# Rows outside, columns inside: another order of the elements in the tiles of h

## The chip, the cores and the metric

The kernel runs on one core of a Trainium2 chip. The metric is the device time of one execution in microseconds (us); lower is better. The kernel before takes 1774.77 us, the median of three runs between 1773.58 and 1776.81 us. Engines are written as in the profile: PE is the matrix engine (PEld its weight loads), DVE the vector engine, ACT the scalar engine, POOL the GpSimd engine, SP the engine whose queue issues most DMAs.

## The reference

Two layers act on x of shape (16, 64, 128, 128), which is 16 images of 64 channels and 128 x 128 pixels.

```python
# layer 0: a Hartley transform cut to 20 x 20 modes, mixed by w1, turned back, blurred, masked
x_ht = dht_2d(x)
out_ht = zeros.at[:, :, :20, :20].set(compl_mul2d(x_ht[:, :, :20, :20], w1))
x = gaussian_smoothing_4d(dht_2d(out_ht) / (H * W)) * mask
# layer 1
h = _group_norm(x, gn1_w, gn1_b)
h = _afno(h, ...) + x            # Fourier transform, 32 x 32 modes, two small layers, back
residual = h
feats = _gelu(_c1(_group_norm(h, gn2_w, gn2_b), fe_w, fe_b))
out = sum over 2 shared layers of _gelu(_c1(feats, shared_w[s], shared_b[s])) / 2
gate_w = top 4 of 16 experts, from feats.mean(axis=(2, 3)) through a small network
for e in range(16):
    out = out + _gelu(_c1(feats, expert_w[e], expert_b[e])) * gate_w[:, e]
return out + residual
```

`_c1` is a 64 x 64 product over the channels, the same for each pixel. The kernel computes only the four experts that each image's gate picks.

## The kernel before

**Ahead of the images.** Layer 0 and the spectrum of layer 1 are worked out in the space of modes, for all 16 images, in about the first 525 us (lines 208 to 658). Nothing there touches h. One table made there matters below: `edges` (line 555) writes, for each image, the 4 rows at either end of a column whose blur is cut by the border; its table `edge` is made on the host in `constant_tables`.

**The images, one after the other.** In the second part, image b goes through these steps, each on tiles of 128 partitions x 2 x 512 numbers of 32 bits. The 128 partitions are 64 channels of the upper and 64 of the lower half of the image's rows; one tile holds 16 columns of 64 rows each, 1024 numbers in a partition, and eight tiles (`NSL`) make an image.

- `columns` (line 713): four calls; PE turns the spectrum into columns in PSUM, and ACT copies it to `u` (line 728). That copy reads PSUM with a step of 64 numbers, 16 at a time, and writes runs of 8.
- `pixels` (line 733): eight calls; PE makes the pixels, one matmul per column (line 744), so that a PSUM tile lies column by column: 16 columns (s, j), with 64 rows i inside. `evacuate` copies it to a tile of `h`. For t in `BY_ACT` = (0, 2, 4, 6) ACT does this (line 754), for the others DVE (line 756). For t below 5 DVE adds the edge rows (line 758); at t = 1 and 3 the DVE copy leaves out the first 4 rows, since line 758 reads them from PSUM itself.
- `feature` (line 804): PE multiplies h by the feature weights (line 814), ACT applies Gelu (line 818).
- `gate` (line 824): a chain of small steps on PE, ACT and DVE from the sums of the features to the four experts' weights; POOL computes the softmax's power (line 877) and fetches the chosen weights with indirect DMAs (line 884).
- `group` / `expert` (line 895): 48 calls for an image, 2 shared layers and 4 experts by eight tiles. PE multiplies (line 904), ACT applies Gelu to a tile `g` (line 909), and DVE adds `g` times its share to `h` in place (line 913). In the last expert (`last`, 8 of the 48) DVE writes the sum to `stg` instead (line 919), a tile of a whole image: [128, 64 rows, 128 columns], row by row as the output has it.
- `store` (line 935): after the last tile of an image SP issues the DMAs that write `stg` out; for the last image this is done after each two tiles. There is one `stg`.

**What sets the order.** PE, ACT and DVE run in the order in which the program issues. That is written out by hand: `PIECES` gives, for each step of image b, its place among the 48 groups of image b and of those before it. So, while the groups of image b run, `columns` (but for its first call, which is among the groups of image b - 1), `pixels` and `feature` of image b + 1 are issued between them. In each group's code the ACT part is put off by one step (`on_act`) and the DVE part by one more (`on_dve`). The buffers: three PSUM tiles `pe` (pool ps2), 13 of `h`, 10 of `f`, 7 of `g`.

The last image's groups have no next image's steps between them.

**The views before.** `evacuate` and the last addition see h and g column by column:

```python
hv, pv = (v.rearrange("p s (j i) -> p (s j) i", i=C) for v in (h, ps))     # line 750
gv, hv = (v.rearrange("p s (j i) -> p (s j) i", i=C) for v in (g, h))      # line 918
box["out"][:, :, c0:c0 + 16].rearrange("p i m -> p m i"),                  # line 920
```

so line 919 reads g and h as they lie and writes 64 rows' elements of one column after another, each 128 numbers (512 bytes) from the one before.

Of the kernel before, what the change touches and what calls it, by code (L numbers as in the profile page):

```python
# [13 lines left out]
ALU = mybir.AluOpType  # L14
# [4 lines left out]
NB, C, N = 16, 64, 128  # L19
K = 20  # L20
# [10 lines left out]
EC = 65  # L31
# [25 lines left out]
def constant_tables():  # L57
# [21 lines left out]
    e1, e2 = blur @ e, mask[:, None] * (blur @ e)  # L79
# [5 lines left out]
    ends = n[:64], np.concatenate([n[124:], n[64:124]])  # L85
# [6 lines left out]
            inv2[r:r + 32, j], inv2[r + 32:r + 64, j] = np.cos(a32)[:, ns], -np.sin(a32)[:, ns]  # L92
    e_cols = np.concatenate([np.stack([s_[:32].reshape(4, 8) for s_ in sides], 1).ravel(), [32]])
    d1 = e1 - g1 * e
    edge = np.zeros((K, K, 2, EC, 4))
    for k2 in range(K):
        for k1 in range(K):
            for j in range(2):
                edge[k2, k1, j] = (np.outer(e2[e_cols, k2], d1[ends[j][:4], k1]).real
                                   - np.outer(e2[e_cols, k2 + 1], d1[ends[j][:4], k1 + 1]).imag)  # L100

# [24 lines left out]
    def by_parity(v):  # L128
        v = v.reshape(K // 2, 2, K, *v.shape[2:])
        return np.ascontiguousarray(np.moveaxis(v, (1, 2, 0), (0, 1, 2)))  # L130
# [6 lines left out]
    def chunked(a):  # L137
        a = a.reshape(4, CH, -1)
        return a.transpose(1, 0, 2)

    sel = np.zeros((CH, K, 2, 32))
    for k1 in range(K):
# [5 lines left out]
    at = np.arange(128)  # L148
# [7 lines left out]
    out = {  # L156
        "fwd1": fwd1,
        "fwd2": fwd2.reshape(N, 2 * K * W1),
        "inv1": inv1.reshape(128, -1),
        "inv2": inv2.reshape(128, -1),  # L160
        "edge": chunked(by_parity(edge).reshape(NM, 2 * EC * 4)).reshape(CH, -1),
        "gain": np.broadcast_to(g1[1:] / g1[:K], (128, K)),
        "spec": chunked(spec.reshape(NM, 2 * MD * MD)),
        "dev": chunked(dev.T.copy()),
# [13 lines left out]
def hartley_afno_moe_kernel(ctx: ExitStack, tc: tile.TileContext, a: dict, out: bass.AP):  # L178
    nc = tc.nc
# [5 lines left out]
    def load(pool, name, shape, eng=None):  # L185
        t = pool.tile(shape, F32, name=name + "_sb", tag=name)
        src = a[name]
        if len(shape) == 3 and len(src.shape) == 2:
            src = src.rearrange("p (a b) -> p a b", b=shape[2])
        (eng or nc.sync).dma_start(t, src)  # L190
        return t
# [16 lines left out]
    with tc.tile_pool(name="modes", bufs=1) as mp:  # L208
# [6 lines left out]
        with tc.tile_pool(name="f_x", bufs=10) as xp, tc.tile_pool(name="f_t", bufs=2) as tp, \  # L215
# [45 lines left out]
            for b in range(NB):  # L261

                t1 = tp.tile([P, 2 * K, C], F32, name="t1")
                for c0 in range(0, C, 8):
                    xt = xp.tile([P, 8, N], F32, name="xt")
                    nc.sync.dma_start(xt, a["x"][b, :, c0:c0 + 8])
                    ps = pp1.tile([P, 8, W1], F32, name="ps1")
# [18 lines left out]
        with tc.tile_pool(name="m_o", bufs=1) as op, tc.tile_pool(name="m_w", bufs=4) as wp, \  # L286
# [16 lines left out]
            edge = load(sc, "edge", [CH, 4, 2 * EC * 4])  # L303
# [7 lines left out]
            for h in range(2):  # L311
                hs_ = slice(h * CL, (h + 1) * CL)
                for ri in range(2):
                    own_rows = slice(h * C + ri * CL, h * C + (ri + 1) * CL)
                    for ro in range(2):
                        c0 = (ri ^ ro) * P + h * CL
# [14 lines left out]
            for k1 in range(K // 2 + 1):  # L331

                ps = pp.tile([P, K // 2, 2, NB, 2], F32, name="psm")
# [15 lines left out]
            for b0 in range(0, NB, 8):  # L349
                for cc in range(2):  # L350
                    pq = [pp2.tile([CH, 8, C], F32, name="pst") for h in range(2)]
                    for i in range(8):
                        for h, (m0, m1) in ((0, (0, C)), (1, (C, CH)), (1, (0, C)), (0, (C, CH))):
                            g = slice(h * C, (h + 1) * C)
# [62 lines left out]
    with tc.tile_pool(name="s_o", bufs=1) as so, \  # L417
# [27 lines left out]
        for g, cols in halves:  # L445
            sq = sqp.tile([CH, 4, 512], F32, name="sq")
            sqs.append(sq)
            for rc in range(4):
                ps = pp2.tile([P, 512], F32, name="psx")
# [17 lines left out]
        gm, gd, gv, y, t = (small(n, HG) for n in ("gm", "gd", "gv", "gy", "gt1"))  # L467
# [36 lines left out]
        for r in range(4):  # L504
            g = slice(r * CL, (r + 1) * CL)
            c0 = (r & 1) * C + (r >> 1) * CL
# [19 lines left out]
        for q in range(4):  # L526
            g = slice(q * 32, (q + 1) * 32)
            i = q % 2 * QB * C
# [98 lines left out]
        for b in range(NB):  # L627
            xk = sw.tile([P, MD * MD], F32, name="xk")
            xr = sw.tile([P, MD * MD], F32, name="xr")
            for n in range(2):  # L630
                cols = slice(n * 512, (n + 1) * 512)
                ps = pp2.tile([P, 512], F32, name="psx")
# [30 lines left out]
    with s3:  # L663
# [14 lines left out]
        def on_act(f):  # L678
            behind_a.append(f)

        def on_dve(f):
            behind_d.append(f)
            while len(behind_d) > 1:
                behind_d.popleft()()
# [5 lines left out]
        def flush():  # L690
            done(0)
            while behind_d:
                behind_d.popleft()()
# [39 lines left out]
        def pixels(box, t):  # L733


            if t == 0:
                if box["columns"] < 4:
                    flush()
                box["h"] = []
            ps = ps2.tile([P, 2, 512], F32, name="pe")  # L740
            for j in range(8):
                for s, half in ((0, 0), (1, 1), (0, 1), (1, 0)):
                    rs = slice(s * C, (s + 1) * C)
                    nc.tensor.matmul(ps[half * C:(half + 1) * C, s, j * C:(j + 1) * C],  # L744
                                     lhsT=u[rs, t * 8 + j], rhs=inv2[rs, half], start=True, stop=True)

            def evacuate():
                h = hpp.tile([P, 2, 512], F32, name="h")
                box["h"].append(h)
                hv, pv = (v.rearrange("p s (j i) -> p (s j) i", i=C) for v in (h, ps))  # L750
                nm = min(16, EC - 16 * t)
                at = 4 if t < 4 and t not in BY_ACT else 0
                if t in BY_ACT:
                    nc.scalar.copy(h, ps)
                else:
                    nc.vector.tensor_copy(hv[:, :, at:], pv[:, :, at:])  # L756
                if nm > 0:
                    nc.vector.tensor_tensor(hv[:, 0:nm, 0:4], (pv if at else hv)[:, 0:nm, 0:4],  # L758
                                            box["edge"].rearrange("p (m i) -> p m i", i=4)[:, 16 * t:16 * t + nm],
                                            ALU.add)  # L760

            on_act(evacuate)

# [133 lines left out]
        def expert(box, t, w, bias, share, last=False):  # L897
            if box["features"] <= t:
                flush()
            f, h = box["f"][t], box["h"][t]  # L900
            ps = ps2.tile([P, 2, 512], F32, name="pe")
            for p, half in ((0, 0), (1, 1), (0, 1), (1, 0)):
                rows_ = slice(p * C, (p + 1) * C)
                nc.tensor.matmul(ps[half * C:(half + 1) * C, p], lhsT=w[rows_],  # L904
                                 rhs=f[rows_, half], start=True, stop=True)

            def activate():
                g = gp.tile([P, 2, 512], F32, name="g")
                nc.scalar.activation(g, ps, AF.Gelu, bias=bias)  # L909

                def add():
                    if not last:
                        nc.vector.scalar_tensor_tensor(h, g, share(), h, ALU.mult, ALU.add)  # L913
                        return
                    if t == 0:
                        box["out"] = stgp.tile([P, C, N], F32, name="stg")
                    c0 = 16 * TILES[t]
                    gv, hv = (v.rearrange("p s (j i) -> p (s j) i", i=C) for v in (g, h))
                    nc.vector.scalar_tensor_tensor(  # L919
                        box["out"][:, :, c0:c0 + 16].rearrange("p i m -> p m i"),  # L920
                        gv, share(), hv, ALU.mult, ALU.add)
                    store(box, t)

                on_dve(add)

            on_act(activate)

        def store(box, t):
            b, o = box["b"], box["out"]
            if b == NB - 1 and t % 2:  # L930
                c0, c1 = 16 * TILES[t - 1], 16 * TILES[t] + 16
            elif b < NB - 1 and t == NSL - 1:
                c0, c1 = 0, N
            else:
                return
            for half, i0, n0, nr in ((0, 0, 0, 64), (1, 4, 64, 60), (1, 0, 124, 4)):
                for r in range(0, nr, 16):
                    e = min(r + 16, nr)
                    nc.sync.dma_start(out[b, :, n0 + r:n0 + e, c0:c1],
                                      o[half * C:(half + 1) * C, i0 + r:i0 + e, c0:c1])  # L940
# [117 lines left out]
```

## Time and profile before

| what | value |
|---|---|
| time, median of 3 runs | 1774.77 us (1773.58 to 1776.81) |
| the profiled execution's own time | 1781.3 us |
| its span, first to last instruction | 1779.5 us |
| instructions | 69874 |
| mean granted PE clock | 0.96 |
| HBM traffic | 109.90 MB read, 87.00 MB written |

The page of the profile gives the busy time of each engine; then groups of instructions of one line, engine and shape with their number, total and mean time, and what ended the idle time before them; then the chain of work that ended last, followed back from the end. The trace behind it can be asked for any stretch of the span: how long each engine was busy there, or what the chain passed through. A matmul's end is modelled, so a busy PE is not a PE at its peak. In a line of a group, "x128 | 255.0, 2037 | 0.0" means 128 instructions, 255.0 us in total, 2037 ns each, and no idle time of the engine just before them.

### The profile page before, as it was taken

The numbers are of one execution on the slowest core, as the hardware profiler recorded it, in microseconds if no ns is written. First come the engines' busy times: TensorE is split into PE (matmuls) and PEld (weight loads), VectorE is DVE, ScalarE is ACT, GpSimd is POOL, SyncE is SP. The second block draws the span as 40 slices with busy tenths as digits, with TensorE's granted clock in tenths as the row PEclk, the third lists the DMA queues.
The fourth block names the chain that finished last, engine by engine and source line by source line (L and its number), as shares of the span: only waits on it lengthen the run. The fifth ranks groups of instructions, "written<-read, shape, count | busy, mean of one in ns | idle before, by whom it ended". The sixth has DMA issues, their size and how long they took to land.

```text
span 1779.5 us, 69874 instructions
## 1 busy us (share of the span) xinstructions
PE 1588.7 (89%) x31752; PEld 821.1 (46%) x31752; DVE 1329.1 (75%) x1668; ACT 1275.8 (72%) x1615; POOL 190.4 (11%) x152
## 2 busy tenths in 40 slices
PE   6778758899988999999999999999999998999984
PEld 6778754233346444544434444444443444444320
DVE  0344334354542899898998989989899898989997
ACT  2233343244554889898988989889898898988985
POOL 0000011000220120202112020120202202021020
PEclk9999969899987999999999999999999999999998
DMA  9999954321542334517254261633616336073145
GB/s 377 315 310 310 279 127 126 82 90 63 153 133 39 41 70 68 116 23 132 47 94 102 37 130 29 115 88 50 128 21 125 81 58 128 11 133 68 35 98 95
DMA packets 296958, 201.42 MB, mean 113 GB/s; under 512 B 259338, under 2 KB 264438, under 8 KB 289614
## 3 DMA queue, kind: packets, MB, share of 16 engines
q1 hardware_dynamic: 292198, 189.60, 45.6%
q0 software_dynamic: 4464, 7.35, 1.6%
q8 instruction: 250, 4.10, 1.0%
q14 instruction: 46, 0.38, 0.1%
HBM read 109.90 MB, written 87.00 MB: 111 GB/s over the span
## 4 chain that ended last, share of the span: by engine, by line
PE 64%; issue 14%; DVE 13%; DMA 4%; ACT 2%; SPq 2%; POOL 0%; DVEq 0%; POOLq 0%; ACTq 0%
PE pe L904 27%; PE pe L721 7%; PE psx L637 7%; PE ps L271 6%; PE pe L744 5%; DVE stg L919 5%; PE pe L814 4%; DVE h L913 3%; PE ps L231 3%; DVE h L756 2%; PE psd L560 2%; DMA spec_sb<-in_spec_dram 1%; PE psd L539 1%; PE pso L586 1%; PE pso L574 1%
## 5 line engine op out<-in xcount | busy, mean ns | idle before, releaser
L909 ACT ACTIVATE g<-pe,wl 128x1024 f32<-128x1024 f32 x512 | 544.9, 1124 | 32.5 <-PE pe L904 18.9
L904 PE MATMUL pe<-f,wl 64*64 64x512 f32 x4096 | 516.6, 606 | 23.9 <-DVE h L756 16.2
L913 DVE SCALAR_TENSOR_TENSOR h<-g,wt,h 128x1024 f32<-128x1024 f32 x384 | 471.7, 1282 | 18.8 <-ACT g L909 17.6
L913 DVE SCALAR_TENSOR_TENSOR h<-g,h 128x1024 f32<-128x1024 f32 x256 | 298.3, 1213 | 18.0 <-ACT g L909 16.9
L909 ACT ACTIVATE g<-pe,vec_sb 128x1024 f32<-128x1024 f32 x256 | 269.1, 1119 | 27.8 <-PE pe L904 23.7
L904 PE MATMUL pe<-f,shw 64*64 64x512 f32 x2048 | 260.6, 618 | 11.0 <-issue 10.0
L919 DVE SCALAR_TENSOR_TENSOR stg<-g,wt,h 128x1024 f32<-128x1024 f32 x128 | 255.0, 2037 | 0.0
L904 PEld LDWEIGHTS pe<-f,wl 64*64 64x64 f32 x4096 | 131.5, 133 | 266.1 <-ACT g L909 96.7
L744 PEld LDWEIGHTS pe<-inv_sb,u 64*64 64x64 f32 x8192 | 151.2, 138 | 109.3 <-issue 43.3
L271 PE MATMUL ps<-fwd_sb,xt 128*64 128x64 f32 x4096 | 154.7, 230 | 41.9 <-issue 35.5
L744 PE MATMUL pe<-inv_sb,u 64*64 64x64 f32 x8192 | 161.6, 224 | 23.3 <-issue 15.3
L877 POOL TENSOR_TENSOR dv<-root_e,dv 128x4 f32<-128x4 f32 x16 | 66.4, 4150 | 1021.7 <-DVE ati L880 908.2
L271 PEld LDWEIGHTS ps<-fwd_sb,xt 128*64 128x64 f32 x4096 | 143.1, 144 | 45.4 <-issue 39.2
L274 ACT COPY t<-ps 128x320 f32<-128x320 f32 x128 | 53.8, 427 | 145.4 <-PE ps L271 145.0
L818 ACT ACTIVATE f<-pe,fba 128x1024 f32<-128x1024 f32 x128 | 145.0, 1144 | 4.9 <-PE pe L814 4.7
L721 PE MATMUL pe<-inv_sb,bmh 52*64 52x33 f32 x4096 | 136.2, 211 | 8.5 <-issue 8.0
L721 PE MATMUL pe<-inv_sb,bmf 64*64 64x64 f32 x4096 | 138.0, 239 | 3.6 <-issue 2.4
L721 PEld LDWEIGHTS pe<-inv_sb,bmf 64*64 64x64 f32 x4096 | 124.3, 140 | 31.3 <-ACT g L909 23.8
L814 PE MATMUL pe<-h,fsa 64*64 64x512 f32 x1024 | 135.4, 608 | 3.6 <-DVE h L758 2.2
L904 PEld LDWEIGHTS pe<-f,shw 64*64 64x64 f32 x2048 | 86.1, 138 | 103.4 <-issue 63.0
L637 PE MATMUL psx<-spec_sb,ot 100*32 100x512 f32 x1024 | 119.4, 608 | 10.7 <-DMA spec_sb<-in_spec_dram 10.7
L721 PEld LDWEIGHTS pe<-inv_sb,bmh 52*64 52x64 f32 x4096 | 123.6, 141 | 10.3 <-issue 9.6
(187 smaller groups left out, 1276.7 us busy)
## 6 DMA issues: line engine op xcount, KB each, us to landing
xt<-in_x_dram SPq DMA_DIRECT2D x128, 512.0 KB
out_dram<-stg SPq DMA_DIRECT2D x105, 512.0 KB
td<-tt SPq DMA_DIRECT2D x16, 512.0 KB
bmf<-td SPq DMA_DIRECT2D x16, 512.0 KB
out_dram<-stg SPq DMA_DIRECT2D x15, 384.0 KB
out_dram<-stg SPq DMA_DIRECT2D x43, 128.0 KB
tnd<-tn SPq DMA_DIRECT2D x32, 128.0 KB
bmf<-td SPq DMA_DIRECT2D x32, 128.0 KB
```

The costliest lines, as they stand in the source:

```text
L271: nc.tensor.matmul(ps[cols, i, :], lhsT=xt[:, i, cols], rhs=fwd1, start=True, stop=True)
L274: nc.scalar.copy(t1[:, :, c0:c0 + 8], src)
L637: nc.tensor.matmul(ps[p0:p0 + CL], lhsT=ot[:, kc, b * C + h * CL:b * C + (h + 1) * CL], rhs=spec[:, kc, ri * 1024 + n * 512:ri * 1024 + (n ...
L721: nc.tensor.matmul(ps[s * C:(s + 1) * C, h, i, 0:at.stop - at.start], lhsT=bmh[rs, c] if part else bmf[rs, c].rearrange("p r m -> p (r m)" ...
L744: nc.tensor.matmul(ps[half * C:(half + 1) * C, s, j * C:(j + 1) * C], lhsT=u[rs, t * 8 + j], rhs=inv2[rs, half], start=True, stop=True)
L814: nc.tensor.matmul(ps[p * C:(p + 1) * C, half], lhsT=fsa[rows_, box["b"]], rhs=box["h"][t][rows_, p], start=True, stop=True)
L818: nc.scalar.activation(f, ps, AF.Gelu, bias=fba[:, box["b"]:box["b"] + 1], accum_out=box["sums"][:, t:t + 1])
L877: nc.gpsimd.tensor_tensor(dv, root_e, dv, ALU.pow)
L904: nc.tensor.matmul(ps[half * C:(half + 1) * C, p], lhsT=w[rows_], rhs=f[rows_, half], start=True, stop=True)
L909: nc.scalar.activation(g, ps, AF.Gelu, bias=bias)
L913: nc.vector.scalar_tensor_tensor(h, g, share(), h, ALU.mult, ALU.add)
L919: nc.vector.scalar_tensor_tensor(box["out"][:, :, c0:c0 + 16].rearrange("p i m -> p m i"), gv, share(), hv, ALU.mult, ALU.add)
```

## The change

The tiles of h, g and f keep their size, but within a tile the 64 rows are now outside and the 16 columns inside.

- The copies from PSUM (lines 754 and 756) write h in this order. They read PSUM with the view "p s (j i) -> p i (s j)": 16 elements with a step of 64 numbers (256 bytes), then the next row.
- The addition of the edge rows (line 758) covers 4 rows of up to 16 columns in place of up to 16 columns of 4 rows; for two tiles of an image one of its inputs is PSUM, read with the same step. The host's table `edge` is put in the matching order.
- The last addition (line 919) writes `stg` in runs of 16 numbers (64 bytes), one per row, and reads g and h as they lie.

Matmuls on h and f, Gelus, the other additions and the DMAs see the same tiles with the pixels in another order; their instructions stay as they are. No instruction, buffer or wait is added or taken away.

```diff
@@ constant_tables
-    edge = np.zeros((K, K, 2, EC, 4))
+    edge = np.zeros((K, K, 2, EC * 4))
...
-                edge[k2, k1, j] = (np.outer(e2[e_cols, k2], d1[ends[j][:4], k1]).real
-                                   - np.outer(e2[e_cols, k2 + 1], d1[ends[j][:4], k1 + 1]).imag)
+                v = (np.outer(d1[ends[j][:4], k1], e2[e_cols, k2]).real
+                     - np.outer(d1[ends[j][:4], k1 + 1], e2[e_cols, k2 + 1]).imag)
+                edge[k2, k1, j, :256] = v[:, :64].reshape(4, 4, 16).swapaxes(0, 1).ravel()
+                edge[k2, k1, j, 256:] = v[:, 64]
@@ pixels / evacuate
-                hv, pv = (v.rearrange("p s (j i) -> p (s j) i", i=C) for v in (h, ps))
+                hv = h.rearrange("p s (i m) -> p (s i) m", m=16)
+                pv = ps.rearrange("p s (j i) -> p i (s j)", i=C)
                 nm = min(16, EC - 16 * t)
                 at = 4 if t < 4 and t not in BY_ACT else 0
                 if t in BY_ACT:
-                    nc.scalar.copy(h, ps)
+                    nc.scalar.copy(hv, pv)
                 else:
-                    nc.vector.tensor_copy(hv[:, :, at:], pv[:, :, at:])
+                    nc.vector.tensor_copy(hv[:, at:], pv[:, at:])
                 if nm > 0:
-                    nc.vector.tensor_tensor(hv[:, 0:nm, 0:4], (pv if at else hv)[:, 0:nm, 0:4],
-                                            box["edge"].rearrange("p (m i) -> p m i", i=4)[:, 16 * t:16 * t + nm],
-                                            ALU.add)
+                    nc.vector.tensor_tensor(hv[:, 0:4, 0:nm], (pv if at else hv)[:, 0:4, 0:nm],
+                                            box["edge"][:, 64 * t:64 * t + 4 * nm]
+                                            .rearrange("p (i m) -> p i m", m=nm), ALU.add)
@@ expert / add
-                    gv, hv = (v.rearrange("p s (j i) -> p (s j) i", i=C) for v in (g, h))
-                    nc.vector.scalar_tensor_tensor(
-                        box["out"][:, :, c0:c0 + 16].rearrange("p i m -> p m i"),
-                        gv, share(), hv, ALU.mult, ALU.add)
+                    gv, hv = (v.rearrange("p s (i m) -> p (s i) m", m=16) for v in (g, h))
+                    nc.vector.scalar_tensor_tensor(box["out"][:, :, c0:c0 + 16], gv, share(), hv,
+                                                   ALU.mult, ALU.add)
```

## The prediction, on record before the result

> **What bounds the kernel now.** I read the page's engine line first, then the groups by shape, then the chain through one image, then the engines' busy time in the same stretch of every image.
>
> ```profile
> PE 1588.7 (89%) x31752; PEld 821.1 (46%) x31752; DVE 1329.1 (75%) x1668; ACT 1275.8 (72%) x1615; POOL 190.4 (11%) x152
> ```
>
> The shares mix the part ahead of the images with the images, so they decide nothing yet. The groups by shape price the operations:
>
> ```profile
> L913 DVE SCALAR_TENSOR_TENSOR h<-g,wt,h 128x1024 f32<-128x1024 f32 x384 | 471.7, 1282 | 18.8 <-ACT g L909 17.6
> L919 DVE SCALAR_TENSOR_TENSOR stg<-g,wt,h 128x1024 f32<-128x1024 f32 x128 | 255.0, 2037 | 0.0
> L754 ACT COPY h<-pe 128x1024 f32<-128x1024 f32 x64 | 64.9, 1014 | 23.4 <-PE pe L744 19.3 <-DMA bmf<-td 2.2 <-PE pe L904 1.8
> L728 ACT COPY u<-pe 128x1024 f32<-128x1024 f32 x64 | 64.8, 1012 | 66.6 <-PE pe L721 51.6 <-PE pe L904 15.0
> L756 DVE COPY h<-pe 128x1024 f32<-128x1024 f32 x32 | 39.2, 1226 | 4.5 <-PE pe L744 4.5
> ```
>
> Lines 913 and 919 are the same operation on the same inputs; only the order of the writes differs, and it costs 2037 - 1282 = 755 ns. "0.0" says that DVE was never idle ahead of line 919: it comes behind a backlog.
>
> The chain through the image from 876 us on stays on DVE from 912.85 to 928.14 us (pieces left out):
>
> ```profile
> 912.85 0.04 DVE h L756
> ...
> 914.14 3.82 DVE stg L919 x2
> ...
> 925.01 0.48 DVE stg L919
> ...
> 926.88 1.26 DVE h L756
> 928.14 0.04 issue
> 928.18 1.95 PE pe L904 x16
> ```
>
> Columns: start, us, what. PE starts its next group only when DVE's copy of h at 926.88 has freed the PSUM tile, and that copy stood behind three writes of stg. This recurs: over the execution PE was idle before line 904 until line 756 for 16.2 us in 30 places.
>
> Last, the 41 us ahead of each image's gate (its first step on DVE, line 829, ends the stretch), for three of 13 images and all together. Columns: us, busy PE, PEld, DVE, ACT, POOL, with the number of instructions, PE clock, DMA share, GB/s.
>
> ```profile
> 826.91:867.91 41.00, 39.91 (x788) 17.25 (x784) 40.75 (x35) 38.73 (x46) 0.00 (x0) 1.00 0.28 36
> 902.09:943.09 41.00, 38.53 (x766) 16.02 (x763) 40.74 (x35) 37.52 (x45) 0.00 (x0) 1.00 0.29 37
> 1278.20:1319.20 41.00, 39.89 (x789) 17.39 (x784) 40.75 (x35) 38.84 (x47) 0.00 (x0) 1.00 0.31 37
> sum 533.00, PE 512.81 PEld 220.54 DVE 527.02 ACT 497.72 POOL 0.00; mean PE 39.45 PEld 16.96 DVE 40.54 ACT 38.29 POOL 0.00
> ```
>
> Here DVE is busy 40.54 of 41 us, 99%, ACT 38.29 (93%). An image takes (1628.13 - 648.65) / 13 = 75.3 us between like points of the chain, so DVE binds for more than half of it. In the rest it does not: from 890 to 900 us PE loses time while the stores run (DMA share 1.04), and at 945 to 960 PE runs without a gap.
>
> In the last image no pixels are interleaved, and DVE alone sets the pace:
>
> ```profile
> 1726.00:1770.50 44.50, 29.72 (x236) 6.03 (x225) 44.38 (x33) 32.26 (x31) 0.00 (x0) 0.91 0.48 82
> ```
>
> [...] line 919 takes 0.755 us / 1024 = 0.74 ns per element more than line 913[...]. For runs, DVE's lines 240 and 243, which read PSUM and write SBUF in runs of 20, take 171 ns for 20 elements and 369 for 200: 1.10 ns per element. [...] no row of this trace has DVE read PSUM with a step and write in runs. [...] eight matmuls of line 904 take 0.86 us in the chain, so PE's 39.45 includes waiting.
>
> **The change, part by part.**
>
> Last addition. Runs of 16 with hops of 512 bytes: I take line 913's 1282 ns. Bounds: not below that, since it is the contiguous form; at worst 2037 as now. DVE loses 0.755 us on each of 128, eight per image. By the table's stretch (groups of line 919 there) six of an image's eight lie in its 41 us; the other two come after the gate, where PE runs without a gap, and I count them as hidden: worth at most 1.5 us an image if PE's cover were gone.
>
> ACT's copies. Line 728 reads PSUM in just the order that line 754 is to have, (s j) inside with a step of 64, and takes 1012 ns against 1014 contiguous, though it writes runs of only 8. So 0.0.
>
> DVE's copies. Four an image. At least 0[...]. [...] I take 0: ACT reads this very pattern from PSUM at 1012 ns for 1024 elements[...].
>
> Edge rows. 64 elements, 225 or 214 ns[...]. Nothing.
>
> No wait, DMA or queue entry is added. The store of an image starts a little earlier; stg is read out by about 900 us and first written again at 914, so that cover of some 14 us stays.
>
> **The sum, per image.** DVE drops by 6 x 0.755 = 4.53 us to 36.0 in the stretch. Next is ACT: 38.29 busy of 41, so no more than 2.7 us are won. From the chain: three writes in its DVE piece, 2.27. From PE's visible idle time: 41 - 39.45 = 1.55. I take 2.0. Fifteen images have a next image's pixels between their groups: 15 x 2.0 = 30.0 us.
>
> **The last image.** DVE is busy 44.38 of 44.5 us, ACT 32.26; eight writes shorten it by 8 x 0.755 = 6.0, and DVE still ends last. Ahead of it, two writes of image 15 (1702.14 and 1705.14 us) stand on DVE before line 876, from where the chain goes to POOL's power (4.29 us) and the indirect DMAs to PE's first expert at 1721.7: 1.5 us. Together 7.5.
>
> Sum: 37.5 us. Against the profiled execution's own 1781.3 that is 1743.8; it lies 0.37% above the median of 1774.8, from which the same sum gives 1737.3, say 1737. What is late next: ACT in the stretch, PE and the stores in the rest.
>
> **Rivals.**
> 1. *As above*, 1737. Own range 1722 (ACT's whole 2.7 us, and a little of the two hidden writes: 15 x 3.0 + 7.5 = 52.5) to 1752 (1.0 an image: 22.5). Chance 0.66.
> 2. *DVE pays the SBUF price for the hopping read*[...]. The copies are what PE waits for. [...] Against: ACT's row. Chance 0.14.
> 3. *The gain is hidden*: ACT and PE, at 93 and 96% in the stretch, take over at once, and only the tail is won: 1774.8 - 7.5 = 1767. For it: these shares. Against: DVE's 99%, and PE's waits for line 756. Chance 0.09.
> 4. *Slower*:[...] It decides from 15 x (4x - 4.53) = 7.5, x = 1.26 us more a copy[...]. For it: DVE's line 542 takes 1212 ns for 512 elements written with a step of 20, over 2 ns each. Against: that is a write to SBUF. Chance 0.08.
> 5. *The runs don't help*: line 919 stays near 2.0 us since each row is still another place; nothing changes, 1775. Against: lines 240 and 243. Chance 0.03.
>
> **How the numbers follow.** A measurement of this kernel tells about 0.2% (3.5 us) from no change. Faster: cases 1 to 3, 0.89, less 0.03 for their edges: 0.86. Slower: case 4 and a little of the others, 0.09. Same: 0.05. For 8 in 10 the range takes in cases 1 to 3 and leaves case 4 out: 1720 to 1768.
>
> **What would show it.** Line 919 near 1.3 us; line 754 still near 1.01 and line 756 near 1.23 us ([...]2.5 and more case 4); DVE's total down by about 97 us; in the stretch ahead of the gate DVE under 95% and ACT near 99%; an image at 73.3 us in place of 75.3; PE's 16.2 us behind line 756 mostly gone. I am wrong if line 756 grows by over 1 us, or if images stay at 75 us with line 919 short.

## The result and the profile after

| what | before | after |
|---|---|---|
| median | 1774.77 us (1773.58 to 1776.81) | 1756.22 us (1754.87 to 1763.34) |
| the profiled execution's own time | 1781.3 us | 1754.87 us |
| its span | 1779.5 us | 1753.1 us |

The kernel became 18.5 us faster: ratio 0.9903, 95% interval 0.9882 to 0.9924. The forecast was 37.5 us, about twice that. The profiled executions differ by 26.4 us, but 8.4 of these lie ahead of the first image's gate (567.5 against 559.1 us), where h isn't touched; from here on a gate is dated by its first matmul on PE, some 2 us behind the first step on DVE that the prediction used. From there to the end it is 18.1 us, which agrees with the medians: 10.4 us over the fifteen images that have a next image between their groups (1126.4 to 1116.0 us from the first to the sixteenth gate, 0.7 an image), and 7.7 us in the tail behind the sixteenth gate (85.6 to 77.9).

First the prices. The groups by shape of the kernel after; the first two numbers behind the bar are us in all and ns of one:

```profile
L922 DVE SCALAR_TENSOR_TENSOR stg<-g,wt,h 128x1024 f32<-128x1024 f32 x128 | 160.4, 1275 | 0.0
L757 ACT COPY h<-pe 128x1024 f32<-128x1024 f32 x64 | 64.9, 1014 | 8.3 <-PE pe L746 6.1 <-DMA bmf<-td 2.2
L759 DVE COPY h<-pe 128x1024 f32<-128x1024 f32 x32 | 39.2, 1224 | 6.4 <-PE pe L746 4.4
```

Lines 922, 757 and 759 are what 919, 754 and 756 were. The addition fell from 2037 to 1275 ns, the price of the contiguous form (1282 on line 913 before, 1278 on line 916 after). The copies cost what they cost before: in these copies a read of PSUM with a step of 256 bytes adds nothing on ACT (1014 and 1014 ns) or on DVE (1226 and 1224).

Then the 41 us ahead of each gate, three of 13 images and all together, with the columns of the view shown before:

```profile
813.43:854.43 41.00, 40.97 (x843) 18.12 (x843) 40.00 (x38) 40.32 (x47) 0.00 (x0) 1.00 0.34 48
888.12:929.12 41.00, 40.97 (x846) 17.66 (x843) 40.20 (x39) 40.43 (x48) 0.00 (x0) 1.00 0.33 41
1259.76:1300.76 41.00, 40.97 (x843) 18.18 (x839) 39.97 (x38) 40.30 (x47) 0.00 (x0) 1.00 0.34 44
sum 533.00, PE 528.55 PEld 230.65 DVE 511.44 ACT 515.01 POOL 0.00; mean PE 40.66 PEld 17.74 DVE 39.34 ACT 39.62 POOL 0.00
```

The engine that binds has changed: PE is busy 40.66 of 41 us, ACT 39.62, and DVE no longer leads. The stretch holds more matmuls than before (843 where there were 788), so it did get shorter. The loss must be somewhere else in the image. The chain through the image from 856 us on, behind its gate, shows where (start us, us, what):

```profile
872.34 3.59 PE pe L907 x32
875.93 0.66 PE pe L723 x36
876.60 0.42 issue
877.01 0.34 PE pe L723 x4
877.36 0.39 issue
877.75 0.33 PE pe L723 x5
878.08 0.39 issue
...
881.07 0.58 PE pe L723 x17
881.66 1.76 PE pe L907 x16
```

This is the fourth `columns` call, 128 short matmuls. From 875.93 to 881.66 it takes 5.7 us; the call at 862.55, ahead of the image's stores, took 2.00. PE stops for some 0.4 us after every few matmuls, and "issue" says that it waits for nothing that the profile shows. Two views of PE's groups, before and then after. Behind the bar: busy us and ns of one; then idle us ahead of the group and what ended it. `u` is read by `pixels`, `bmf` and `bmh` by `columns`:

```profile
L904 PE MATMUL pe<-f,wl 64*64 64x512 f32 x4096 | 516.6, 606 | 23.9 <-DVE h L756 16.2 <-DMA wl<-exd,ati 4.7 <-ACT g L909 1.5
L744 PE MATMUL pe<-inv_sb,u 64*64 64x64 f32 x8192 | 161.6, 224 | 23.3 <-issue 15.3 <-ACT u L728 7.8
L721 PE MATMUL pe<-inv_sb,bmf 64*64 64x64 f32 x4096 | 138.0, 239 | 3.6 <-issue 2.4 <-ACT o L589 1.2
L721 PE MATMUL pe<-inv_sb,bmh 52*64 52x33 f32 x4096 | 136.2, 211 | 8.5 <-issue 8.0
```

```profile
L907 PE MATMUL pe<-f,wl 64*64 64x512 f32 x4096 | 511.3, 606 | 6.8 <-DMA wl<-exd,ati 3.9 <-issue 1.8 <-ACT f L821 0.4
L746 PE MATMUL pe<-inv_sb,u 64*64 64x64 f32 x8192 | 153.7, 221 | 5.7 <-issue 4.5 <-ACT u L730 1.1
L723 PE MATMUL pe<-inv_sb,bmf 64*64 64x64 f32 x4096 | 151.6, 238 | 12.6 <-issue 11.0 <-ACT o L591 1.2
L723 PE MATMUL pe<-inv_sb,bmh 52*64 52x33 f32 x4096 | 146.7, 211 | 18.6 <-issue 17.5
```

The 16.2 us behind DVE's copies are gone, and busy and idle together the expert tiles take 518.1 us in place of 540.5. But `columns`, the two lower groups, takes 329.5 us where it took 286.3, and `pixels` gives only 25.5 of that back (159.4 for 184.9). The idle time with nothing waited for has grown from 25.7 to 33.0 us over these groups (15.3 + 2.4 + 8.0; 4.5 + 11.0 + 17.5) and has moved to `columns`. The busy time of the same 4096 matmuls differs too (138.0 and 151.6 us), so both columns have to be read.

For the experiments I read one more stretch, matmul by matmul: from the start of the four shared tiles ahead of the fourth `columns` call to the first expert tile behind the third `pixels` call. The expectations call its end "the eighth expert tile". Here it is called **the stretch after the gate**. It took 20.85 us before and 21.44 after (means of 13 images). All other gains and losses of an image are small: PE won 0.98 and 0.46 us, 1.44 together, at the two places where it had waited for DVE's copies.

### The profile page after: what moved, and what is told of

The parts are those of the page before. It is cut to its first block, busy times and chain, and to the rows that moved or that the text cites. A ratio compares the mean times of both kernels' runs of the same rounds, so it can differ in the third digit from the quotient of the medians.

```text
span 1753.1 us, 69874 instructions
## 1 busy us (share of the span) xinstructions
PE 1588.3 (91%) x31752; PEld 819.3 (47%) x31752; DVE 1249.8 (71%) x1668; ACT 1268.8 (72%) x1615; POOL 169.1 (10%) x152
## 4 chain that ended last, share of the span: by engine, by line
PE 82%; issue 7%; DMA 4%; DVE 4%; ACT 2%; SPq 1%; POOL 0%; POOLq 0%; DVEq 0%; ACTq 0%
PE pe L907 38%; PE pe L723 8%; PE pe L746 7%; PE pe L817 7%; PE psx L639 7%; PE ps L273 6%; PE ps L233 2%; PE psd L562 2%; DMA spec_sb<-in_spec_dram 1%; PE psd L541 1%; PE pso L588 1%; DVE h L916 1%; PE pso L576 1%; DMA fwd_sb<-in_fwd_dram 1%; DMA edge_sb<-in_edge_dram 1%
## 5 line engine op out<-in xcount | busy, mean ns | idle before, releaser
L907 PE MATMUL pe<-f,wl 64*64 64x512 f32 x4096 | 511.3, 606 | 6.8 <-DMA wl<-exd,ati 3.9
L916 DVE SCALAR_TENSOR_TENSOR h<-g,wt,h 128x1024 f32<-128x1024 f32 x384 | 471.9, 1278 | 44.3 <-ACT g L912 43.0
L746 PEld LDWEIGHTS pe<-inv_sb,u 64*64 64x64 f32 x8192 | 146.2, 137 | 87.6 <-ACT g L912 49.2
L723 PE MATMUL pe<-inv_sb,bmh 52*64 52x33 f32 x4096 | 146.7, 211 | 18.6 <-issue 17.5
L723 PE MATMUL pe<-inv_sb,bmf 64*64 64x64 f32 x4096 | 151.6, 238 | 12.6 <-issue 11.0
L922 DVE SCALAR_TENSOR_TENSOR stg<-g,wt,h 128x1024 f32<-128x1024 f32 x128 | 160.4, 1275 | 0.0
L746 PE MATMUL pe<-inv_sb,u 64*64 64x64 f32 x8192 | 153.7, 221 | 5.7 <-issue 4.5
L723 PEld LDWEIGHTS pe<-inv_sb,bmf 64*64 64x64 f32 x4096 | 129.8, 138 | 44.8 <-ACT g L912 23.7
L723 PEld LDWEIGHTS pe<-inv_sb,bmh 52*64 52x64 f32 x4096 | 129.2, 139 | 24.9 <-issue 24.3
L880 POOL TENSOR_TENSOR dv<-root_e,dv 128x4 f32<-128x4 f32 x16 | 34.1, 2131 | 1029.0 <-DVE dv L879 967.3
L730 ACT COPY u<-pe 128x1024 f32<-128x1024 f32 x64 | 64.7, 1012 | 91.0 <-PE pe L723 91.0
```

What stands on the lines that cost most here:

```text
L723: nc.tensor.matmul(ps[s * C:(s + 1) * C, h, i, 0:at.stop - at.start], lhsT=bmh[rs, c] if part else bmf[rs, c].rearrange("p r m -> p (r m)" ...
L730: nc.scalar.copy(dst, ps.rearrange("p h i n -> p n h i"))
L922: nc.vector.scalar_tensor_tensor(box["out"][:, :, c0:c0 + 16], gv, share(), hv, ALU.mult, ALU.add)
```

## The experiments

Each ratio is against the kernel before, measured beside it on the same chip; differences of two experiments are of medians from one chip.

**Stores left out, e1 and e2.** Hypothesis: `stg` is ready 1.5 us earlier (10.33 in place of 11.83 us after the gate), so the stores start earlier and run into PE's short matmuls.

```diff
-            elif b < NB - 1 and t == NSL - 1:
+            elif b < 1 and t == NSL - 1:
```

> The kernel after without the stores of images 1 to 14 (their part of the output is left out; images 0 and 15 are stored). Theory A: the relief of DVE is worth some 1.4 us an image, and 0.6 of it is lost again because the stores of an image now start 1.5 us earlier and so stall PE's instructions in the fourth columns call. Then without stores PE's idle time with nothing waited for goes, an image falls from 74.5 to about 71.5 us and the kernel to about 1714 us. Theory B: ACT and PE simply take over from DVE and the stores have no part in it: 1750 to 1756 us.

> The kernel before without the stores of images 1 to 14 (left out of the output in the same way). Theory A: the difference to the kernel after without stores is the whole relief, 15 x 1.4 + 7.7 = 29 us or more, since DVE then has no stall of PE in which to catch up. Theory B: the difference stays at 18 us.

After without stores: 1737.26 us, ratio 0.9761 (0.972 to 0.9801). Before without stores: 1757.94 us, 0.9887 (0.9852 to 0.9922). The difference, 20.7 us, is hardly more than the 18.5 with stores. In e1 the fourth `columns` call still takes 4.6 us, in e2 it takes 1.9. Earlier stores alone are not the cause.

**Stores later, e3.** The stores of images 0 to 12 were to be issued behind the next load of `bmf`, in `spectrum`. `send` holds the loop of `dma_start` that `store` had.

```diff
...
+            if b < NB - 3:
+                unsent.append(send)
+            else:
+                send()
```

> The kernel after with the stores of images 0 to 12 issued behind the first load of bmf, which waits for PE's fourth columns call: they begin some 13 us later. Theory A: the columns and the first pixels run at full speed, an image takes 73 us or less, and the kernel 1735 to 1745 us. Theory B: 1756 us, or more if the next image's first write of stg has to wait for the stores.

1758.42 us, 0.9874 (0.9844 to 0.9903). The trace shows the stores starting 10.36 us after the gate, just as in the kernel after, so the edit moved nothing and this run tells only how well the kernel after repeats.

**The two writes behind the gate as they were, e4.** Only the last two writes of `stg` of images 0 to 14 go column by column again.

```diff
+                    if t >= NSL - 2 and box["b"] < NB - 1:
+                        to, gv, hv = (v.rearrange("p i m -> p m i") for v in (to, gv, hv))
```

> The kernel after, but the last two writes of stg of images 0 to 14 go column by column again, so that they take 2.0 us or more and the stores start as late as in the kernel before. Theory A: slower writes make a faster kernel, 0.6 us an image, about 1747 us. Theory B: no gain, 1756 to 1760 us.

1751.3 us, 0.9826 (0.9793 to 0.986): giving DVE more work made the median 7.1 us lower than e3's, though the intervals overlap. The two writes take 2.14 to 2.29 us here, a little more than the 2.04 before; here g and h are read with hops as well. The `columns` call is at 2.0 us and the stretch after the gate at 20.81. This speaks for a price of the prediction's "hidden" writes, but doesn't show it alone.

**Plain loads of the weights, e5 and e6.** The gathers behind POOL's power also come 3 us earlier (18.1 in place of 21.0 us after the gate). Here each image loads experts 0 to 3 by plain DMAs from ACT's queue; the choice of experts is left out.

```diff
-                nc.gpsimd.indirect_dma_start(out=wl, ...)
+                for hf in range(2):
+                    nc.scalar.dma_start(wl[hf * C:(hf + 1) * C], exd[k])
```

> The kernel after, with the four indirect gathers of expert weights on POOL replaced by eight plain DMAs from ACT's queue that always fetch experts 0 to 3 (the choice of experts is left out). Theory C: PE's stall follows the gathers; they start 3 us earlier after the change, since POOL's power is held up less by DVE, and so hit the columns call. Then the fourth columns call falls from 4.6 to 1.9 us, the calls from it to the eighth expert tile take some 2.2 us less, and the kernel some 1723 us. Theory A (the stores stall PE): the columns call stays at 4.6 us and the time at 1756 us.

> The kernel before with the same plain loads (experts 0 to 3, the choice left out). Theory C: without the gathers the change is worth only what the copies of h won, 15 x 1.44 + 7.7 = 29 us more than in the run after with plain loads: about 1752 us. Theory A: 18 us more than that run, whatever that is.

After: 1933.44 us, 1.0933 (1.0904 to 1.0963). Before: 1964.07 us, 1.111 (1.1079 to 1.1142). The loads queued behind the stores and PE stood for some 14 us an image (211.0 / 15), which the groups of e5 show:

```profile
L906 PE MATMUL pe<-f,shw 64*64 64x512 f32 x2048 | 278.4, 655 | 211.2 <-ACT g L911 211.0
L911 ACT ACTIVATE g<-pe,vec_sb 128x1024 f32<-128x1024 f32 x256 | 272.0, 1122 | 239.3 <-DMA out_dram<-stg 209.0 <-issue 13.8 <-PE pe L906 9.3
```

PE waited for ACT's g, and ACT for the queue. The pair is still of use: its difference is 30.6 us, and behind such a stand the short matmuls of e5 have 8.4 us of idle time with nothing waited for (0.5 ahead of `pixels`, 7.9 ahead of `columns`), where the kernel after has 33.0. But the stand itself could be the reason, so the pair doesn't settle the cause.

**The fourth `columns` call two places earlier, e7, and two of ACT's copies given to DVE, e8.**

```diff
-            (columns, (-55, -48, -44, -38))     # e7
+            (columns, (-55, -48, -44, -40))
-BY_ACT = (0, 2, 4, 6)                           # e8
+BY_ACT = (0, 4)
```

In e8 DVE makes six of an image's eight copies and ACT two.

> The kernel after with the fourth columns call two groups earlier (place -40 for -38), so that it runs ahead of the gathers' stretch. Theory C: the call takes 1.9 us, the stall falls on calls with few instructions, and an image is 0.6 to 1.5 us shorter: 1735 to 1747 us. Theory A: the stores have begun by then as well, so there is no gain: 1756 us.

> The kernel after with two of ACT's four copies of h given to DVE (BY_ACT = 0 and 4). If ACT is what paces the stretch ahead of the gate now, it loses 2 x 0.9 us there and an image is 1.0 to 1.8 us shorter: about 1735 us. If PE does, nothing is won (1756 us); and if DVE's backlog returns, the PE waits for its copies come back and it is slower than 1760 us.

e7: 1751.3 us, 0.9913 (0.9879 to 0.9948), no gain over the kernel after's 0.9903; the call takes 3.5 us at its new place. e8: 1775.21 us, 1.0044 (1.0029 to 1.006): all of the gain is lost. The change took 6 x 0.76 = 4.6 us off DVE in the stretch ahead of the gate, and 2 x 1.22 us put back on it are enough to make PE wait for it again: 13.0 us ahead of `pixels` behind DVE's copies. But the idle time with nothing waited for is larger too, 30.6 us ahead of `pixels`, so DVE is not the whole of the loss.

**Neither stores nor gathers, with plain loads, e9; gathers later and earlier, e10 and e11; the kernel after once more, e12.** e9 is e1 and e5 together; e10 and e11 move the gate step that issues the gathers among the groups.

```diff
-            (step("gate", gate), (-5, -3, -2, -1, 0, 1, 6, 9)),
+            (step("gate", gate), (-5, -3, -2, -1, 0, 1, 8, 11)),     # e10
+            (step("gate", gate), (-5, -3, -2, -1, 0, 1, 2, 9)),      # e11
```

> The kernel after without the stores of images 1 to 14 and with plain loads of experts 0 to 3 from ACT's queue (both left out of the result as in the runs before). In the run without stores alone the fourth columns call still took 4.5 us. Theory C (the gathers stall PE): without them it takes 1.9 us, an image about 70 us, the kernel below 1700 us. Theory D (neither stores nor gathers, but something else at that place, such as PE's own instructions): the call stays at 4.5 us and the kernel at 1735 us.

> The kernel after with the gate's step that ends in the gathers put two groups later (places 8 and 11 for 6 and 9), so that they start at some 20 us after the gate's first step, as in the kernel before, while the stores start early as after the change. Theory C: the columns call falls from 4.6 to 1.9 us, the stall hits the first pixels call, an image is 0.6 us shorter, the kernel 8 to 10 us below the kernel after of the same call. Theory A or D: no change of the columns call, the same time.

> The kernel after with that step four groups earlier (place 2), so that the gathers run some 5 us earlier, beside expert tiles with few instructions. Theory C: both the columns call (1.9 us) and the first pixels call (1.0 us) are spared and an image is 1.5 us shorter or more: 20 us below the kernel after of the same call, unless PE now waits for DVE's ranking of the experts. Theory D: no gain.

> The kernel after once more, as the measure for the two runs beside it on the same chip: 0.990 of the kernel before, by every theory.

e9: 1773.64 us, 1.0028 (1.0008 to 1.0048). PE stood 5.7 us longer at the shared tiles for the weights; behind that the `columns` call took 2.2 us. Again a stand hides the question. e10: 1749.78 us, 0.9888 (0.9819 to 0.9957). e11: 1760.51 us, 0.9948 (0.9929 to 0.9967). e12: 1750.73 us, 0.9905 (0.987 to 0.9939). Gathers 2.8 us later changed nothing that can be told; 5 us earlier cost some 0.4%, with intervals that just overlap. And e12 corrected my reading. It is the kernel after, but in its profiled execution the fourth `columns` call takes 2.5 us in the mean, not 4.8, and it is long in every third image only. **Which call the stops fall on differs between executions of one program.** What stays is the sum: the stretch after the gate takes 21.16 us in e12 and 21.44 in the first profile.

**No gathers, e13 and e14; two writes alone, e15; no gathers and two writes as before, e16.** To take the gathers out without a wait in their place, images 1 to 15 use the weights that image 0 fetched.

```diff
-            box["wl"] = []
-            for k in range(TOPK):
+            box["wl"] = [] if box["b"] == 0 else boxes[0]["wl"]
+            for k in range(TOPK if box["b"] == 0 else 0):
```

e15 is the kernel before with only the last two writes of images 0 to 14 in runs of 16; e16 is e14 with e4's edit.

```diff
+                    if t >= NSL - 2 and box["b"] < NB - 1:
+                        to = box["out"][:, :, c0:c0 + 16]
+                        gv, hv = (v.rearrange("p s (i m) -> p (s i) m", m=16) for v in (g, h))
```

> Leaves out the gathers of the weights for images 1 to 15: they use the weights that image 0 fetched, and nothing waits for a load. Stores stay. If it is the gathers that hold PE back after the gate (about 2.8 of the 4.0 us per image that PE loses between the shw tiles and the eighth expert tile, as the run without stores has it), this runs about 15 x 2.8 = 42 us under before, some 1730 us. If PE's stall at the columns and pixels calls has another cause (POOL's power, DVE's writes, the stores), it stays, and the time is within 10 us of before.

> The same without gathers in the kernel after. Theory (what is given back per image is PE held for longer by gathers that come 3 us earlier): the give-back goes, and the difference to e13 is the whole relief, 15 x 1.5 + 7.7 = 30 us. Rival (the give-back comes from the earlier stores, from POOL's shorter power or from DVE itself): the difference stays at 18 to 21 us. In the trace the columns call should take 1.8 to 2.2 us in both kernels under the theory.

> The kernel before with only the last two writes of stg of images 0 to 14 in runs of 16 (their elements go to wrong places: the order inside these two slices is left out); everything ahead of the gate as before. The prediction counted such writes as hidden: 0 to 1.5 us faster. Theory: they alone make the kernel slower, by 0.3 to 0.75 us x 15 = 4 to 11 us, as DVE, POOL's power and the gathers come earlier after the gate; the power falls from 4.3 to 2.0 us and the gathers begin near 18 instead of 21 us after the gate.

> The kernel after without gathers and with the last two writes of stg of images 0 to 14 column by column. With gathers the two slow writes made the kernel some 5 to 10 us faster. Theory (they did so by holding the gathers back): without gathers nothing is left to gain, and it is within 3 us of e14, or slower. Rival (the slow writes help by the later stores or by the long power): again 5 to 10 us faster than e14.

e13: 1772.89 us, 0.9979 (0.996 to 0.9998). e14: 1754.16 us, 0.9867 (0.9846 to 0.9887). Their difference is 18.7 us: **the theory of the gathers falls**. e16: 1739.23 us, 0.9809 (0.9775 to 0.9843), 14.9 us below e14. So the slow writes help without gathers too. The stores, which they hold back by 1.9 us, are the likely way; POOL's power, which is long again in e16 (4.27 us), was not separated from them. e15: 1788.13 us, 1.006 (1.004 to 1.008), 11 us *slower* than before. Its profiled execution, at 1774.18 us, was the fastest of nine, so the groups of e15 show where time goes and not how much is lost:

```profile
L923 DVE SCALAR_TENSOR_TENSOR stg<-g,wt,h 128x1024 f32<-128x1024 f32 x128 | 232.1, 1860 | 0.0
L744 PE MATMUL pe<-inv_sb,u 64*64 64x64 f32 x8192 | 152.6, 221 | 5.7 <-issue 3.2 <-ACT g L909 1.4 <-ACT u L728 1.1
L721 PE MATMUL pe<-inv_sb,bmf 64*64 64x64 f32 x4096 | 151.1, 239 | 13.7 <-issue 11.9 <-ACT o L589 1.2
L721 PE MATMUL pe<-inv_sb,bmh 52*64 52x33 f32 x4096 | 148.6, 213 | 13.5 <-issue 12.8
```

DVE has 255.0 - 232.1 = 22.9 us less to do, and the kernel is slower. Busy and idle together, `columns` takes 326.9 us in place of before's 286.3, `pixels` 158.3 in place of 184.9: 14.0 us more for the same matmuls. So the loss is there by itself, without the relief at DVE's copies.

**Neither stores nor gathers, no wait in their place, e17 and e18.** Taking either away left the loss; this pair takes both, by the edits of e1 and e13.

> Leaves out both the gathers of the weights of images 1 to 15 (they use those of image 0) and the stores of images 1 to 14. Theory now (either stream of transfers holds PE back after the gate, and one is enough; with PE's stand of 4 us or more the loss is taken up): without both and without a wait in their place the 4.0 us per image between the shw tiles and the eighth expert tile are gone, and this runs 40 to 60 us under before. Rival (PE loses the time for a reason of its own after a dense run of short matmuls, whatever the transfers do): the loss stays at 2 to 3 us per image, and the time is within 25 us of before.

> The same in the kernel after. Theory (transfers): nothing is left that can be given back, and it is 15 x 1.5 + 7.7 = 30 us faster than e17, with the columns call at 1.8 to 2.0 us in both. Rival (PE's own): the difference stays at 18 to 21 us as in the pairs without stores and without gathers, and the columns call again takes over 3 us in this kernel and under 2.2 in e17.

Before: 1727.1 us, 0.972 (0.9693 to 0.9747). After: 1692.95 us, 0.953 (0.9504 to 0.9557). The difference is 34.2 us, near the 37.5 that the prediction had. PE's groups, e17 and then e18:

```profile
L904 PE MATMUL pe<-f,wl 64*64 64x512 f32 x4096 | 517.8, 605 | 31.3 <-DVE h L756 16.6 <-DVE h L758 6.9 <-ACT g L909 4.3
L744 PE MATMUL pe<-inv_sb,u 64*64 64x64 f32 x8192 | 147.3, 220 | 3.6 <-issue 2.4 <-ACT u L728 1.2
L721 PE MATMUL pe<-inv_sb,bmf 64*64 64x64 f32 x4096 | 133.0, 235 | 2.9 <-issue 1.7 <-ACT o L589 1.2
L721 PE MATMUL pe<-inv_sb,bmh 52*64 52x33 f32 x4096 | 131.8, 208 | 4.7 <-issue 4.3 <-DMA bmh<-ond 0.4
```

```profile
L907 PE MATMUL pe<-f,wl 64*64 64x512 f32 x4096 | 509.7, 603 | 4.0 <-ACT u L730 0.8
L746 PE MATMUL pe<-inv_sb,u 64*64 64x64 f32 x8192 | 148.0, 221 | 3.5 <-issue 2.2 <-ACT u L730 1.1
L723 PE MATMUL pe<-inv_sb,bmf 64*64 64x64 f32 x4096 | 137.8, 238 | 3.0 <-issue 1.7 <-ACT o L591 1.2
L723 PE MATMUL pe<-inv_sb,bmh 52*64 52x33 f32 x4096 | 134.3, 210 | 4.7 <-issue 4.3 <-DMA bmh<-ond 0.3
```

The "issue" of 25.7 and 33.0 us is down to 8.4 and 8.2: in these runs PE's stops beside `columns` and `pixels` come with transfers, and one of the two streams is enough (39.7 us in e13 and 46.5 in e14 with the stores alone; 27.1 at `columns` alone in e1, with the gathers). With the stops gone, the change takes 31.3 - 4.0 = 27.3 us of waits away from the expert tiles: the 16.6 behind DVE's copies, and 6.9 behind the edge rows at line 758, which don't show in the kernels with transfers; there PE gets to that place some 3.5 us later, which would explain it. Over the fifteen images the gates of these two profiles move together by 28.0 us (1077.95 to 1049.95). By the same measure the change wins 10.4 us with both streams, 9.6 with the stores alone (e13 and e14) and 19.2 with the gathers alone (e2 and e1). These are single profiles, and the medians of the two pairs hardly differ (18.7 and 20.7 us), so which stream costs more stays open.

These two profiles hold a check of their own, since the stores of image 0 are left in and run in the second image. There the stretch after the gate takes 20.3 us in e17 and 20.8 in e18, in the images behind it 17.2 and 16.4.

All kernels that bear on it, means of 13 images from the traces (the second to the fourteenth; for e17 and e18 that includes the second); "column" and "run" tell how the last two writes of `stg`, behind the gate, are made:

| kernel | stores | gathers | last two writes | fourth columns call, us | stretch after the gate, us |
|---|---|---|---|---|---|
| before | yes | yes | column | 2.06 | 20.85 |
| after (e12) | yes | yes | run | 4.77 (2.48) | 21.44 (21.16) |
| e4 | yes | yes | column | 1.96 | 20.81 |
| e15 | yes | yes | run | 5.02 | 21.33 |
| e2 / e1 | no | yes | column / run | 1.85 / 4.57 | 19.95 / 19.65 |
| e13 / e14 | yes | no | column / run | 2.18 / 3.07 | 20.52 / 21.20 |
| e16 | yes | no | column | 2.15 | 20.05 |
| e17 / e18 | no | no | column / run | 1.84 / 1.84 | 17.37 / 16.77 |

## Why the prediction was right and wrong

**Right.** *Last addition*: 1275 ns against 1282 taken. *ACT's copies* and *DVE's copies*: nothing, as taken; rivals 2 and 4, which gave DVE's hopping read a price that no trace of the kernel before showed, are out, and so is rival 5. *The last image*: 7.5 us forecast, 7.7 in the profiles. *What is late next*: ACT and PE took over in the stretch, as forecast. *The relief of 2.0 us an image*: near, once no transfers stand in its way. e17 and e18 differ by 28.0 / 15 = 1.87 in their profiles, and by (34.2 - 7.7) / 15 = 1.77 in their medians. With the transfers PE won 1.44 at DVE's copies, near the 1.55 that the prediction read as PE's visible idle time, and less than the 2.0 that it took.

**Wrong.** The step that failed is "the other two come after the gate, where PE runs without a gap, and I count them as hidden". They are on no path that sets the end, so their gain was put at no less than nothing. They cost. Two writes that are 0.76 us shorter let `stg` be ready 1.5 us earlier, so the stores start at 10.36 in place of 11.86 us after the gate; the gate's steps on DVE and POOL's power end earlier too, and the gathers start at 18.1 in place of 21.0. PE's short matmuls stay where they were, near 19 us after the gate, and lose more time beside these transfers (in the first profiles 4.77 us for the fourth `columns` call in place of 2.06).

The stretch after the gate shows the price. Without transfers the change makes it 0.60 us shorter (17.37 to 16.77). With them it makes it 0.59 longer, or 0.31 by e12. So 0.9 to 1.2 us an image are missing there; by the medians it is (34.2 - 18.5) / 15 = 1.05. Half or more of this, 0.60, is relief that isn't had while transfers hold PE up, and the rest is time lost. e15 shows a loss alone (11 us), and e4 and e16, with the two writes slow again, are 7.1 and 14.9 us below e3 and e14. For the fifteen images together: 30.0 us forecast, 15 x 1.44 = 21.6 won at DVE's copies, some 11 lost behind the gate (by e15's median), 10.4 kept.

The prediction had the sign of it in hand: it named that "PE loses time while the stores run", and that the store "starts a little earlier". It asked only whether `stg` would still be free in time, and not what the earlier transfers would meet.

Rival 3, that the gain ahead of the gate is hidden, is not what happened: PE did win its 1.44 us there.

**What PE waits for.** The kept traces answer a good part of this. The page of the profile has a queue that carries instructions:

```profile
q8 instruction: 250, 4.10, 1.0%
```

(packets, MB, share of 16 engines; 4.10 MB / 250 is 16.4 KB a packet, and PE's 31752 matmuls / 250 make 127 to a packet.) The packed trace has the start and length of every packet. In the 20 profiles, between the second gate and the last, PE stops 243 times for over 0.7 us with nothing waited for. Every one of these stops ends 1.15 to 1.61 us after a packet of q8 has landed, though such packets come only every 6 to 8 us on average. The stops also fall on the same matmuls again and again, within one kernel multiples of about 127 apart: one is at matmul 25485 of the execution in twelve profiles, one at matmul 12131 in eleven. I read these stops as PE waiting for its next instructions; the traces show the times of the packets, and no run tested this by itself.

With neither stores nor gathers there are 2 such stops (3.8 us in e17 and in e18), both in the second image and none behind it. There are 13 (24.3 us) in the kernel before, 12 (15.3 us) after and 20 (45.7 us) in e12: these stops come beside the transfers.

**What stays open.** Shorter stops, of some 0.4 us as in the chain above, are of another kind: they don't keep that distance from a landed packet (before and after, their ends lie anywhere from 0.03 to 7.4 us behind one). They appear only in kernels with gathers. Of these, before, e2 and e4, with the two writes by column, have 15 to 24, and after, e1, e3 and e15, with the two writes in runs, 47 to 50; but e8 and e10 to e12, measured on other chips than e1 to e4 and e15, have none, and e7 has one. In the first pair of profiles it is this kind that grew, from 5.4 us before to 19.3 after. What PE waits for in them isn't shown, nor whether the chip decides which kind comes. And transfers don't always cost: the first image has gathers and no stores beside it, and its stretch takes 21.1 us in the first profile after but 16.6 in e12.

## What to carry to other kernels

Faster work on an engine that has slack still moves what it releases. For each such edit ask which transfers start earlier, and what the binding engine is doing at that moment: here two shorter writes that nobody waited for cost about half of what the other six won. The order of a tile could be turned for nothing in its copy from PSUM (1014 ns for 1014 on ACT, 1224 for 1226 on DVE), and that was paid back where SBUF is written (1275 for 2037). When an engine stops and waits for nothing that the profile shows, compare the ends of its stops with the landings of the instruction packets (here all 243 ended 1.15 to 1.61 us behind one). And a stall's place in one profile is not its cause: the same program showed it at another call the next time, so read the sum over the stretch, and take away both of two suspects before clearing either.

## What the runs showed of the hardware

- In these copies a PSUM read with a step of 256 bytes cost neither ACT nor DVE anything: 1014 and 1224 ns for 1024 elements, 1014 and 1226 where the same elements were read as they lie.
- POOL's power of 512 numbers takes 4.3 us in nearly every image before, and mostly 2.05 after, by the trace of the tile `dv` (minimum, median and maximum ns), before and then after:

```profile
L877 POOL TENSOR_TENSOR dv<-root_e,dv x16: 2055/4283/4359, 582.3 to 1711.9; 128x4 f32<-128x4 f32 x16
```

```profile
L880 POOL TENSOR_TENSOR dv<-root_e,dv x16: 1032/2052/4283, 574.7 to 1690.6; 128x4 f32<-128x4 f32 x16
```

  It goes with DVE's last two writes of `stg`: e4, with both long again, has 4.29 us, and e15, where they alone are short, has 2.13 in the mean of the 16 (4.15 before).
- With stores, gathers or both, a stretch of PE's work that takes 17 us with neither takes 2.6 to 4.7 us longer (the table above).
- All 243 of PE's stops of over 0.7 us with nothing waited for end 1.15 to 1.61 us after a packet of 16.4 KB has landed on the queue of instructions.
